# Stage 3 of a four-stage network: pairs finished one step on, merges two turns on, copies out of PSUM on ScalarE, the substitution of diagonal blocks on GpSimd

## The chip, the cores and the metric

The kernel runs on one core of a Trainium2 chip. The metric is the device time of one execution in microseconds (us), the median of several. A profile of one execution, taken by the hardware profiler, stands beside it. The engines are PE (TensorE matmuls; PEld are its weight loads), DVE (VectorE), ACT (ScalarE), POOL (GpSimd) and SP (SyncE, which here issues nearly all DMAs). Each engine works through its own queue in order.

## What is computed

The network has two layers of two blocks each, all in float32, on 2048 tokens of width 512 (4 sequences of 512): a state-space block, a mixture of experts, a gated delta rule ("stage 3", all that is changed here), and a sequence-routed mixture. Stage 3, cut to what matters:

```python
q = silu(conv(x @ Wq))            # causal depthwise conv of 4 taps
k = silu(conv(x @ Wk)) * D ** -0.5
v = silu(conv(x @ Wv))            # 16 heads of 128
alpha, beta = sigmoid(x @ Wa + ba), sigmoid(x @ Wb + bb)
def step(St, inp):                # one token; the state is 128x128 a head
    q_, k_, v_, a_, b_ = inp
    err = einsum('bhij,bhj->bhi', St, k_) - v_
    Sn = a_ * St - b_ * err * k_  # outer product of err and k_
    return Sn, einsum('bhij,bhj->bhi', Sn, q_)
o = layernorm(o) * ln_w + ln_b    # each head apart
o = o * sigmoid(x @ Wg)
y = o @ Wo
x = x + layernorm(y)
```

## The kernel before

The kernel computes the recurrence in chunks of 128 tokens. A **step** of stage 3 is one pair of heads of one sequence of 512 tokens (4 chunks): 8 pairs times 4 sequences are 32 steps, and the loop at the end of `delta_rule` runs once more to drain. Inside a chunk the recurrence is a triangular system; its 128x128 matrix is inverted by blocks of 32. The pieces, generators that give up control at each `yield`, are:

- `prepare(h, ...)`, once a head: the projections k, q and v (`project`, L151: each four products over the 512 inputs, which the trace shows as eight MATMULs of 512 columns), each followed by `conv_silu` (L156 to L163): ACT writes the last tap and the bias to `cv`, DVE adds three taps reading the projection `p` in PSUM (L158), ACT takes the sigmoid (L162), POOL multiplies (L163). Then come the masked products `lt` and `pt` (L672, L675), and the diagonal blocks of `lt` go to DRAM (L679); last `kq`, `gc` and `kt` (L685 to L694).
- `solve(blocks, yi)`: all 32 diagonal blocks of the pair (2 heads, 4 chunks, 4 blocks) come back from DRAM laid out over 128 partitions (`lb`, L710), are inverted by forward substitution, 31 rounds of a multiply (L720, into `term`) and an add (L727, into `xb`), and go by DRAM into `yi` (L732, L736).
- `merge(lts, yi)`: from the inverted diagonal blocks to the whole inverse. Three DVE transposes of `yi` (L752 to L754), then four rounds of small products on PE (L760, L772 and L780, L793, L801), each followed by copies.
- `recur(heads, yi, o)`: for each of the 4 chunks, products in PSUM tag `sq` (L817): `r` (copied out by ACT, L830), `u` (copied out by DVE, L840), the new state `S` (DVE, L847 and L850), the output `o` (ACT, L858).
- `finish(o, ...)`, not a generator: statistics of `o` (DVE L114 and L115, POOL L117 and L118), `normalise` (DVE, L122), then for each head the gate projection (L151, from `wg`), its sigmoid `gt` (L892), four PE transposes of `o` (L895), scaling into `oT` (L897) and the product with `gt` (POOL, L898), then 16 MATMULs with `wo` (L903) whose sums are added to `y` (L909).

Step n of the loop issues `prepare` of pair n (both heads) in turns with `merge` of pair n-1, then `solve` of pair n in turns with `recur` of pair n-1, and then `finish` of pair n-1 as a whole. After a sequence's last pair, `residual` (statistics, `normalise`, POOL addition, L147) follows.

The order on each engine's queue is not the program's. It is fixed when the program is built, by a planner that takes instructions as their inputs and buffers come free by its own estimates, and prefers the earlier in the program among those. A tile's buffers are shared by tag, `bufs` of them: PSUM has three for `mm` (projections, `lt`, `pt`, gates, `wo` sums), three for `tr` (transposes, merges) and two for `sq` (the recurrence). `cv` and `sg` have two buffers each, `o` and `gt` one. The two inverses `yi0` and `yi1` take turns, and `lt`, `pt`, `vT`, `kq`, `kt` and `gc` have four buffers, two pairs' worth.

Of the kernel before, what the change touches and what calls it, by code (L numbers as in the profile page):

```python
# [16 lines left out]
P = 128  # L17
# [59 lines left out]
def network(ctx: ExitStack, tc: tile.TileContext, a: dict, out: bass.AP):  # L77
# [75 lines left out]
    def conv_silu(pool, dst, p, w, bias):  # L153

        cv = pool.tile([P, S], F32, tag="cv", name="cv", bufs=2)
        nc.scalar.activation(cv, p, AF.Identity, bias=bias, scale=w[:, 3:4])  # L156
        for j in range(1, 4):
            nc.vector.scalar_tensor_tensor(  # L158
                cv[:, j:], p[:, : S - j], w[:, 3 - j : 4 - j], cv[:, j:], ALU.mult, ALU.add
            )  # L160
        sg = pool.tile([P, S], F32, tag="sg", name="sg", bufs=2)
        nc.scalar.activation(sg, cv, AF.Sigmoid)  # L162
        nc.gpsimd.tensor_tensor(dst, cv, sg, ALU.mult)  # L163
# [417 lines left out]
    def delta_rule():  # L581
        with (
# [22 lines left out]
            def decays(xT):  # L605

                zp = ps("sq")[:H2, :]
                project(zp, lambda k: wab[:, k, 0:H2], xT)
                al = bp.tile([H2, TPB, CP], F32, tag="al", name="al")
                nc.gpsimd.memset(al[:, :, 0:1], 0.0)  # L610
                nc.scalar.activation(al[:, :, 1:], chunk(zp), AF.Sigmoid, bias=ba)
                ga = bp.tile([H2, TPB * CP], F32, tag="ga", name="ga")
                flat = al.rearrange("h c t -> h (c t)")
                nc.vector.tensor_tensor_scan(ga, flat, c("pad1")[:H2], 0.0, ALU.mult, ALU.add)
                dd = dram.tile([2, H2, TPB * CP], F32, tag="dd", name="dd")
                nc.sync.dma_start(dd[0], flat)
                nc.sync.dma_start(dd[1], ga)
                bps = ps("sq")[:, : TPB * H2]
                for i in range(TPB):
                    dst = bps[:, i * H2 : (i + 1) * H2]  # L620
                    for k in range(KD):
                        nc.tensor.matmul(
                            dst,
                            lhsT=xT[:, k, i * P : (i + 1) * P],
                            rhs=wab[:, k, H2:],
                            start=k == 0,
                            stop=False,
                        )
# [5 lines left out]
                nc.vector.tensor_scalar(nb, nb, -1.0 / P, None, ALU.mult)  # L634
                return dd, nb

            def prepare(h, w, xT, dd, nb, blocks, out):
# [5 lines left out]
                for j, dst in ((1, qk[:, 0, :]), (0, qk[:, 1, :]), (2, vT)):  # L643
                    p = ps("mm")
                    project(p, lambda k: w[:, k, j, :], xT)
                    conv_silu(sp, dst, p, cw[:, j, h, :], cb[:, j, h : h + 1])
                    yield
# [56 lines left out]
            def solve(blocks, yi):  # L704
# [11 lines left out]
                for i in range(BK - 1):  # L716
# [3 lines left out]
                    nc.vector.tensor_tensor(  # L720
# [6 lines left out]
                    nc.vector.tensor_tensor(rest, rest, term, ALU.add)  # L727
# [10 lines left out]
            def merge(lts, yi):  # L738
# [10 lines left out]
                lo, hi = slice(0, 2 * BK), slice(2 * BK, P)  # L749
                xx = sp.tile([P, UNITS, 2 * BK], F32, tag="xx", name="xx", bufs=1)  # L750
# [56 lines left out]
            def recur(heads, yi, o):  # L807

                st = None
                for cc in range(TPB):  # L810
# [29 lines left out]
                    nc.vector.tensor_copy(  # L840
# [40 lines left out]
            def finish(o, ws, wos, pair, xT, y):  # L881
# [5 lines left out]
                gated = []  # L887
                for j in range(2):
                    p = ps("mm")
                    project(p, lambda k: ws[j][:, k, :], xT)  # L890
                    gt = sp.tile([P, S], F32, tag="gt", name="gt", bufs=1)
                    nc.scalar.activation(gt, p, AF.Sigmoid)  # L892
                    p = ps("tr")
# [4 lines left out]
                    nc.gpsimd.tensor_tensor(oT, oT, gt, ALU.mult)  # L898
                    gated.append(oT)
                for i in range(TPB):  # L900
# [7 lines left out]
                    else:  # L908
                        nc.vector.tensor_tensor(y[i], y[i], p, ALU.add)  # L909

# [14 lines left out]
            before = None  # L925
            for n in range(B * NPAIR + 1):
                b, pair = divmod(n, NPAIR)
                now, parts, heads = None, [], []
                if n < B * NPAIR:
                    if pair == 0:  # L930
# [3 lines left out]
                        y = [  # L934
                            bp.tile([P, D], F32, tag=f"y3{i}", name=f"y3{i}") for i in range(TPB)
                        ]
# [9 lines left out]
                    now = (heads, inverses[n % 2], b, pair, xT, y)  # L946
# [246 lines left out]
```

## Time and profile before

| quantity | value |
|---|---|
| time, median of 3 runs | 3653.46 us (3652.5 to 3656.45) |
| the profiled execution | 3652.81 us, of which span 3651.0 us |
| busy in the span | PE 3179.4, PEld 1752.8, DVE 2064.8, ACT 799.0, POOL 953.5 us |
| one regular step of stage 3 (1987.2 to 2052.2) | 65.0 us: PE 59.27, DVE 44.88, ACT 15.86, POOL 19.74 busy |
| the next step (2052.2 to 2117.1) | 64.9 us: PE 59.18, DVE 44.82, ACT 15.87, POOL 19.73 busy |
| three steps round a change of sequence (1639 to 1857) | 147.0 and 71.0 us |
| mean granted clock of TensorE | 0.907 |

The span runs from the first to the last instruction. Stage 3 begins before 1200 us (the first MATMUL with `wh` is at 1190.2) and its last output `o` is written at 3366. A busy time is a sum of instruction durations; a PE that waits with an instruction started still counts as busy. The granted clock is the share of full clock that the chip gave TensorE in a stretch.

### The profile page before, as it was taken

The numbers are of one execution on the slowest core, as the hardware profiler recorded it, in microseconds if no ns is written. First come the engines' busy times: TensorE is split into PE (matmuls) and PEld (weight loads), VectorE is DVE, ScalarE is ACT, GpSimd is POOL, SyncE is SP. The second block draws the span as 40 slices with busy tenths as digits, with TensorE's granted clock in tenths as the row PEclk, the third lists the DMA queues.
The fourth block names the chain that finished last, engine by engine and source line by source line (L and its number), as shares of the span: only waits on it lengthen the run. The fifth ranks groups of instructions, "written<-read, shape, count | busy, mean of one in ns | idle before, by whom it ended". The sixth has DMA issues, their size and how long they took to land.

```text
span 3651.0 us, 39495 instructions
## 1 busy us (share of the span) xinstructions
PE 3179.4 (87%) x13779; PEld 1752.8 (48%) x13779; DVE 2064.8 (57%) x5189; ACT 799.0 (22%) x1399; POOL 953.5 (26%) x1018
## 2 busy tenths in 40 slices
PE   7889989899995889989989989889899989897268
PEld 3333344455552455555555645555555545555123
DVE  4556441311125667676766666766676767664852
ACT  2223211111110222222222222222222222221111
POOL 1322120300016323322423222323223323221112
PEclk9889989999997889989989989989999989998679
DMA  6000010389973322322322322323322323220300
GB/s 239 0 1 0 0 50 0 137 285 319 319 262 93 81 63 60 90 60 54 82 63 64 89 59 53 83 60 80 73 60 64 78 60 77 69 60 22 107 12 35
DMA packets 281240, 316.23 MB, mean 87 GB/s; under 512 B 119073, under 2 KB 184993, under 8 KB 281042
## 3 DMA queue, kind: packets, MB, share of 16 engines
q1 hardware_dynamic: 266496, 277.62, 26.7%
q10 hardware_dynamic: 9426, 19.31, 1.4%
q0 software_dynamic: 5120, 16.78, 1.4%
q8 instruction: 110, 1.80, 0.2%
q14 instruction: 88, 0.72, 0.1%
HBM read 271.95 MB, written 41.68 MB: 86 GB/s over the span
## 4 chain that ended last, share of the span: by engine, by line
PE 75%; DVE 12%; POOL 6%; issue 3%; ACT 3%; DMA 2%; SPq 0%; POOLq 0%; ACTq 0%; DVEq 0%
PE mm L151 32%; PE sq L817 7%; PE mm L903 7%; PE mm L512 5%; PE mm L672 3%; PE sq L534 3%; PE sq L276 2%; POOL rs L118 2%; PE tr L358 2%; PE sq L1086 2%; DVE o L122 2%; DVE prod L997 2%; DVE term L720 1%; DVE st L114 1%; DVE xb L727 1%
## 5 line engine op out<-in xcount | busy, mean ns | idle before, releaser
L151 PE MATMUL mm<-xT,wh 128*128 128x512 f32 x1536 | 691.2, 607 | 2.2 <-DVE cv L158 2.0
L158 DVE SCALAR_TENSOR_TENSOR cv<-mm,prm,cv 128x511 f32<-128x511 f32 (+2 forms) x672 | 499.3, 744 | 289.2 <-ACT cv L156 275.1
L151 PEld LDWEIGHTS mm<-xT,wh 128*128 128x128 f32 x1536 | 294.4, 194 | 364.8 <-issue 357.6
L903 PE MATMUL mm<-wo,oT 128*128 128x512 f32 x512 | 293.9, 738 | 60.0 <-POOL oT L898 60.0
L156 ACT ACTIVATE cv<-mm,prm 128x512 f32<-128x512 f32 x224 | 172.6, 771 | 524.1 <-PE mm L151 516.7
L720 DVE TENSOR_TENSOR term<-lb,xb 128x60 f32<-128x60 f32 (+24 forms) x992 | 257.7, 260 | 20.5
L151 PE MATMUL mm<-xT,wg 128*128 128x512 f32 x512 | 262.2, 600 | 0.7 <-ACT gt L892 0.7
L727 DVE TENSOR_TENSOR xb<-xb,term 128x60 f32<-128x60 f32 (+24 forms) x992 | 223.7, 226 | 24.7
L903 PEld LDWEIGHTS mm<-wo,oT 128*128 128x128 f32 x512 | 120.0, 242 | 216.8 <-issue 139.2
L163 POOL TENSOR_TENSOR qk<-cv,sg 128x512 f32<-128x512 f32 x128 | 162.5, 1269 | 201.5 <-ACT sg L162 201.4
L895 PE MATMUL tr<-const,o 128*128 128x128 f32 x256 | 101.8, 467 | 111.9 <-DVE o L122 111.1
L162 ACT ACTIVATE sg<-cv 128x512 f32<-128x512 f32 x224 | 140.4, 627 | 256.6 <-DVE cv L158 255.6
L512 PE MATMUL mm<-gu,rT 128*128 128x352 f32 x624 | 190.9, 459 | 0.2 <-ACT rT L508 0.2
L151 PE MATMUL mm<-xT,gu 128*128 128x512 f32 (+1 forms) x384 | 176.2, 618 | 12.6 <-DVE act L353 12.6
L512 PEld LDWEIGHTS mm<-gu,rT 128*128 128x128 f32 x624 | 118.2, 190 | 76.5 <-issue 17.8
L817 PE MATMUL sq<-S,kq 128*128 128x128 f32 x768 | 154.5, 283 | 0.0
L117 POOL TENSOR_SCALAR rs<-mv 128x1 f32<-128x1 f32 (+2 forms) x112 | 30.9, 276 | 449.1 <-DVE mv L115 448.9
L672 PE MATMUL mm<-qk 128*128 128x128 f32 x1024 | 137.8, 283 | 6.3 <-POOL vT L163 2.9
L276 PE MATMUL sq<-w_out,G 128*128 128x512 f32 x256 | 128.0, 651 | 13.4 <-POOL G L272 11.7
L546 POOL DMA_INDIRECT got<-yg,index x32 | 38.1, 1189 | 362.5 <-DMA yg<-yo 345.4
L163 POOL TENSOR_TENSOR vT<-cv,sg 128x512 f32<-128x512 f32 x64 | 100.2, 1565 | 115.3 <-ACT sg L162 115.3
L672 PEld LDWEIGHTS mm<-qk 128*128 128x128 f32 x1024 | 123.9, 194 | 11.0 <-POOL vT L163 3.1
(231 smaller groups left out, 4891.2 us busy)
## 6 DMA issues: line engine op xcount, KB each, us to landing
gu<-in_gu SPq DMA_DIRECT2D x86, 704.0 KB
wh<-in_wh SPq DMA_DIRECT2D x64, 768.0 KB
ag<-dd SPq DMA_DIRECT2D x64, 516.0 KB
dn<-in_dn SPq DMA_DIRECT2D x43, 512.0 KB
wg<-in_wg SPq DMA_DIRECT2D x64, 256.0 KB
wo<-in_wo SPq DMA_DIRECT2D x64, 256.0 KB
lb<-blocks SPq DMA_DIRECT2D x128, 128.0 KB
xg<-zero SPq DMA_DIRECT2D x3, 3328.0 KB
```

What stands on the lines that cost most here:

```text
L151: nc.tensor.matmul(dst, lhsT=w(k), rhs=xT[:, k, :], start=k == 0, stop=k == n - 1)
L156: nc.scalar.activation(cv, p, AF.Identity, bias=bias, scale=w[:, 3:4])
L158: nc.vector.scalar_tensor_tensor(cv[:, j:], p[:, : S - j], w[:, 3 - j : 4 - j], cv[:, j:], ALU.mult, ALU.add)
L162: nc.scalar.activation(sg, cv, AF.Sigmoid)
L163: nc.gpsimd.tensor_tensor(dst, cv, sg, ALU.mult)
L276: nc.tensor.matmul(po, lhsT=G[ct][:, i * P : (i + 1) * P], rhs=w_out[:, ct, :], start=ct == 0, stop=ct == NCT - 1,)
L512: nc.tensor.matmul(dst, lhsT=rT[:, k, :], rhs=gu[:, k, lo : lo + F], start=k == 0, stop=k == KD - 1)
L672: nc.tensor.matmul(one(p, cc), lhsT=one(kT, cc), rhs=one(rhs, cc), start=True, stop=True)
L720: nc.vector.tensor_tensor(term, lb[:, i : i + 1, i + 1 :].to_broadcast([P, n, left]), xb[:, :n, i : i + 1].to_broadcast([P, n, left]), ALU ...
L727: nc.vector.tensor_tensor(rest, rest, term, ALU.add)
L817: nc.tensor.matmul(p[:, j, :], lhsT=lhsT, rhs=rhs, start=n == 0, stop=n == len(terms) - 1,)
L903: nc.tensor.matmul(p, lhsT=one(gated[j], i), rhs=wos[j], start=j == 0, stop=j == 1)
```

## The change

It does six things to stage 3 and nothing to the others:

1. `finish` becomes a generator that starts a step later. In step n it takes part, first in each turn, in the phase of `prepare` of pair n and `merge` of pair n-1, for pair n-2: a turn for each gate projection, one for the transposes and products, two for the `wo` sums, with the `residual` of a sequence's last pair inside them. The statistics and the normalisation of `o` (`centred`) stay at the end of the step. The loop runs once more, `o` and `gt` get two buffers, and the loads of `wg` and `wo` are issued after those of `wh`.
2. `merge` gives up its first two turns.
3. `conv_silu` in stage 3 (`apart=True`) first copies the projection out of PSUM by ACT into the `sg` buffer; the three DVE taps read that copy, and the sigmoid overwrites it afterwards.
4. The copy of `u` goes from DVE to ACT.
5. The 31 multiplies and 31 adds of the substitution go from DVE to POOL.
6. For room, `al` and `ga` of `decays` share the two `xn` buffers, and the four `y` tiles are taken when a sequence's first pair is finished.

```diff
-    def conv_silu(pool, dst, p, w, bias):
+    def conv_silu(pool, dst, p, w, bias, apart=False):
         cv = pool.tile([P, S], F32, tag="cv", name="cv", bufs=2)
+        sg = pool.tile([P, S], F32, tag="sg", name="sg", bufs=2)
+        if apart:
+            nc.scalar.copy(sg, p)
+            p = sg
         nc.scalar.activation(cv, p, AF.Identity, bias=bias, scale=w[:, 3:4])
...
-        sg = pool.tile([P, S], F32, tag="sg", name="sg", bufs=2)
         nc.scalar.activation(sg, cv, AF.Sigmoid)
...
-                al = bp.tile([H2, TPB, CP], F32, tag="al", name="al")
+                al = bp.tile([H2, TPB, CP], F32, tag="xn", name="al", bufs=2)
...
-                ga = bp.tile([H2, TPB * CP], F32, tag="ga", name="ga")
+                ga = bp.tile([H2, TPB * CP], F32, tag="xn", name="ga", bufs=2)
...
-                    nc.vector.tensor_tensor(
+                    nc.gpsimd.tensor_tensor(
                         term,
...
-                    nc.vector.tensor_tensor(rest, rest, term, ALU.add)
+                    nc.gpsimd.tensor_tensor(rest, rest, term, ALU.add)
...
                 lo, hi = slice(0, 2 * BK), slice(2 * BK, P)
+                for _ in range(2):
+                    yield
                 xx = sp.tile([P, UNITS, 2 * BK], F32, tag="xx", name="xx", bufs=1)
...
-                    nc.vector.tensor_copy(
+                    nc.scalar.copy(
                         u, pair(lambda j, vT, pt, kq, gc, kt: [(yi[:, j * TPB + cc, :], r[:, j, :])])
...
-            def finish(o, ws, wos, pair, xT, y):
+            def centred(o):
                 rows = [(cc, j) for cc in range(TPB) for j in range(2)]
                 mv, rs = stats([o[:, cc, j, :] for cc, j in rows], EPS / P, "o")
                 for n, (cc, j) in enumerate(rows):
                     normalise(o[:, cc, j, :], o[:, cc, j, :], mv, rs, n)
-                gated = []
+
+            def finish(o, ws, wos, b, pair, xT, y):
+                gates = []
                 for j in range(2):
                     p = ps("mm")
                     project(p, lambda k: ws[j][:, k, :], xT)
-                    gt = sp.tile([P, S], F32, tag="gt", name="gt", bufs=1)
+                    gt = sp.tile([P, S], F32, tag="gt", name="gt", bufs=2)
                     nc.scalar.activation(gt, p, AF.Sigmoid)
+                    gates.append(gt)
+                    yield
+                gated = []
+                for j in range(2):
                     p = ps("tr")
...
-                    nc.gpsimd.tensor_tensor(oT, oT, gt, ALU.mult)
+                    nc.gpsimd.tensor_tensor(oT, oT, gates[j], ALU.mult)
                     gated.append(oT)
+                yield
                 for i in range(TPB):
...
+                    if pair == NPAIR - 1:
+                        residual(bp, b * TPB + i, y[i])
+                    if i % 2:
+                        yield
...
-            before = None
-            for n in range(B * NPAIR + 1):
+            before = last = None
+            for n in range(B * NPAIR + 2):
...
                 if before:
-                    gates = gate_weights(before[3])
                     parts.append(merge([head[0] for head in before[0]], before[1]))
+                if last:
+                    if last[2] == 0:
+                        y = [
+                            bp.tile([P, D], F32, tag=f"y3{i}", name=f"y3{i}") for i in range(TPB)
+                        ]
+                    o, at, of, x_of = last
+                    parts.insert(0, finish(o, *gate_weights(of), at, of, x_of, y))
                 in_turns(*parts)
-                parts = []
+                parts, last = [], None
...
-                    o = sp.tile([P, TPB, 2, P], F32, tag="o", name="o", bufs=1)
+                    o = sp.tile([P, TPB, 2, P], F32, tag="o", name="o")
                     parts.append(recur([head[1] for head in before[0]], before[1], o))
                 in_turns(*parts)
                 if before:
-                    finish(o, *gates, *before[3:])
-                    if before[3] == NPAIR - 1:
-                        for i in range(TPB):
-                            residual(bp, before[2] * TPB + i, before[5][i])
+                    centred(o)
+                    last = (o, *before[2:])
                 before = now
```

More of the change, by code (lines that the diff above doesn't have):

```diff
@@ L645, in prepare @@
                     project(p, lambda k: w[:, k, j, :], xT)
-                    conv_silu(sp, dst, p, cw[:, j, h, :], cb[:, j, h : h + 1])
+                    conv_silu(sp, dst, p, cw[:, j, h, :], cb[:, j, h : h + 1], apart=True)
                     yield
@@ L933, in delta_rule @@
                         dd, nb = decays(xT)
-                        y = [
-                            bp.tile([P, D], F32, tag=f"y3{i}", name=f"y3{i}") for i in range(TPB)
-                        ]
                     blocks = dram.tile([2, TPB, NB, BK, BK], F32, tag="blocks", name="blocks")
@@ L945, in delta_rule @@
                         parts.append(prepare(h, w, xT, dd, nb, blocks[j], heads))
-                    now = (heads, inverses[n % 2], b, pair, xT, y)
+                    now = (heads, inverses[n % 2], b, pair, xT)
                 if before:
-                    gates = gate_weights(before[3])
                     parts.append(merge([head[0] for head in before[0]], before[1]))
+                if last:
[5 more added lines that the diff above has]
+                    parts.insert(0, finish(o, *gate_weights(of), at, of, x_of, y))
                 in_turns(*parts)
-                parts = []
+                parts, last = [], None
                 if now:
```

## The prediction

> **What bounds the kernel now.** I read the page's busy line first, then the busy times of stretches of one regular step of stage 3, then the timeline where PE goes idle, then the groups by shape.
>
> ```profile
> PE 3179.4 (87%) x13779; PEld 1752.8 (48%) x13779; DVE 2064.8 (57%) x5189; ACT 799.0 (22%) x1399; POOL 953.5 (26%) x1018
> core 0: us, PE busy (x) PEld busy (x) DVE busy (x) ACT busy (x) POOL busy (x), PEclk, DMA share, GB/s
> 1987.20:2034.40 47.20, 46.79 (x299) 29.93 (x297) 30.68 (x76) 13.31 (x25) 15.26 (x16) 1.00 0.41 98
> 2034.40:2038.00 3.60, 0.18 (x3) 0.02 (x1) 1.79 (x12) 0.50 (x2) 1.90 (x2) 0.88 0.02 6
> 2038.00:2043.10 5.10, 3.21 (x9) 1.45 (x9) 4.93 (x20) 1.47 (x3) 1.26 (x1) 0.50 0.01 3
> 2043.10:2047.40 4.30, 4.30 (x5) 1.84 (x6) 3.69 (x13) 0.57 (x1) 1.31 (x1) 0.50 0.00 0
> 2047.40:2052.20 4.80, 4.80 (x13) 2.11 (x12) 3.79 (x14) 0.00 (x0) 0.00 (x0) 1.00 0.00 0
> ```
>
> Columns: stretch, length, then busy us of PE, PEld, DVE, ACT, POOL, the granted clock, the DMA share. The reader is to see that PE is the limit for 47.2 us of the 65.0 (46.79 busy, full clock), and that the other 17.8 us are `finish`: 3.6 us idle, then 9.4 us at half clock, then the rest. The timeline (start, length, what; in brackets the idle time before and what ended it) names the waits:
>
> ```profile
> 2035.88 1.67 POOL L118 TENSOR_TENSOR rs<-rs,mhalf 128x8 f32<-128x8 f32 x1
> 2037.99 3.24 PE L895 MATMUL tr<-const,o 128*128 128x128 f32 x8 [3.42 <-DVE o L122]
> 2043.09 1.22 PE L903 MATMUL mm<-wo,oT 128*128 128x512 f32 x1 [1.87 <-POOL oT L898]
> 2041.78 1.26 POOL L898 TENSOR_TENSOR oT<-oT,gt 128x512 f32<-128x512 f32 x1 [4.23 <-ACT oT L897]
> 2041.91 1.22 DVE L720 TENSOR_TENSOR term<-lb,xb 128x75 f32<-128x75 f32 x1
> ```
>
> PE waits for statistics and normalisation (3.42), paces its transposes by DVE (3.24), waits for the product with the gate (1.87). The last two lines are another fact: a DVE multiply of two SBUF inputs, 0.21 us alone, takes 1.22 when a POOL product has just begun, and ends with it.
>
> ```profile
> L118 POOL TENSOR_TENSOR rs<-rs,mhalf 128x8 f32<-128x8 f32 x32 | 53.3, 1666 | 2.7
> L651 POOL TENSOR_TENSOR d<-const,nb 128x516 f32<-128x516 f32 x64 | 67.1, 1049 | 130.2 <-DVE nb L634 70.2 <-DVE m L658 60.1
> L689 POOL COPY gc<-ag 128x4 f32<-128x4 f32 x64 | 12.0, 188 | 249.7 <-DVE S L850 233.0 <-DMA ag<-dd 15.0 <-DVE term L720 0.2
> L117 POOL TENSOR_SCALAR rs<-mv 128x8 f32<-128x8 f32 x32 | 7.7, 240 | 255.5 <-DVE mv L115 255.5
> L131 ACT COPY xT<-tr 128x512 f32<-128x512 f32 x48 | 27.1, 587 | 226.0 <-PE tr L130 225.7
> ```
>
> These rows (total busy, mean ns, idle before) are my prices for operations that move.
>
> [...] 0.50 follows the idle 3.42 us in every step I looked at. [...] L651 gives 1049/516 = 2.0, and I use that.
>
> **The change, part by part, for a regular step of 65.0 us.**
>
> *Finish a step later, with two `gt`.* The work stays the same: 8 transposes and 16 `wo` MATMULs. In the full-clock stretch 128-column MATMULs start 0.11 us apart and 512-column ones 0.43, so they need 8 x 0.11 + 16 x 0.43 = 7.8 us against 17.8 now: a **gain of 10.0**, leaving PE 47.2 + 7.8 = **55.0 us**. The gate projections already lie inside `recur` in this trace and only change place; under `recur` the next step's first projections can lie, since `mm` has three buffers. The normalisation, 8 x 0.34 us of DVE and 1.9 of POOL, is no longer waited for by PE but still blocks DVE's queue (taps, `lt` behind it) if POOL answers late. The loads of `wg` and `wo`, 4 of 256 KB, pass behind `wh` on SP; they were waiting for their buffers anyway, and about 40 us of cover remain: 0, and if it went, at most some us.
>
> *Copies on ACT.* Six copies of 587 ns (L131) and four of 372 instead of DVE's 422: ACT goes from 15.9 to 15.9 + 3.5 + 1.5 = 20.9 us: hidden, far under 55. PSUM is free earlier, but the copy now waits for one of two `sg` buffers, which POOL's product frees. `u` on ACT can queue behind a 0.77 us activation; four times, up to 3 us on `recur`'s chain, hidden while PE has projections to do, 0 to 3 if not. DVE loses 1.7.
>
> *The taps* now have two SBUF inputs: 18 a step at 0.747 = 13.4 us[...].
>
> *Substitution on POOL.* It leaves DVE: (257.7 + 223.7)/32 = 15.0 us a step; DVE falls to 44.9 - 15.0 - 1.7 = 28.2. On POOL it is 62 dependent instructions. The elements are the sum of (i//4+1)(31-i) over 31 rounds = 1560, so 50 an instruction. None this small with two inputs is in the trace. Low: 0.188 of the 4-element copy and nothing for elements but 0.05: 0.24. High: L118, whose 1, 4 and 8 elements take 571, 1040 and 1666, has 0.41 fixed, plus 50 x 2.0 ns: 0.51. I take 0.20, between L689 and L117, plus 0.10 = **0.30**: 18.6 us a step.
>
> [...] POOL's other work is 18.8 us a step (medians: four products of 1.26 for `qk`, two for `vT`, two for `oT`, 4 x 0.90, 2 x 1.05, 1.9, and 1.1 of small ones). DVE's holders are 13.4 of taps, two scans of 1.22 and 8 normalisations of 0.34 = 18.6. Sum 18.8 + 18.6 + 18.6 = **56.0**; before it was 18.8 + 5.2 + 12.8 = 36.8. With 3 us for hand-overs and queues standing at a wait (POOL's for `sg`, for `lb` to land), **59.0 us**. That is above PE's 55.0[...].
>
> *Merges two turns on.* Nothing is added; the inverse gets about two projections' turns more to arrive. Today the chain is: blocks leave at 2017.6, the substitution starts at 2029.95 and ends at 2054.1, `xx` is transposed at 2061.8, so 12.3 + 24.1 + 7.7 us. On POOL the middle becomes 62 x 0.38 (0.08 between two dependent POOL instructions, L117 to L118) = 24 alone, 35 to 45 with other POOL work[...]. Behind a late `xx` stand the taps on DVE and everything on PE. With two buffers of `yi` there is room for it: 0.
>
> *`al`, `ga` in `xn`, `y` late, residual inside `finish`.* Four times in all; the 147 + 71 us round a change of sequence are 23 above three regular steps. The residual's waits get cover: 0 to 8 us gained each of three times, a small loss possible if `al` waits for `xn`; I take 10 in all.
>
> **Sum.** The last pair's finish stays bare, so 31 x (65.0 - 59.0) = 186, plus 10: 196. From the profiled 3652.8 (span 3651.0 and 1.8 around it; the median of runs is 0.7 higher): 3652.8 - 196 + 0.7 = about **3458 us**.
>
> **The rivals.**
>
> *A, PE stays the bound* (0.22). If a small POOL instruction costs 0.24, [...] PE's 55.0 rules: 31 x 10.0 + 10 gives 3333. [...] Against it: 55.0 leaves no slack for any wait.
>
> *B, POOL's substitution delays the inverse: slower* (0.24). Place: between `lb` and L752. If the planner queues `merge` before the next pair's `lt`, a period is 12.3 + substitution + 7.7 + some 8 for the merge; it passes 65 once the substitution spans over 37 us. The same comes[...] once an instruction costs over (65.0 - 3 - 37.4)/62 = 0.40. At a span of 39, 67 us a step: + 62, so 3715[...]. For it: in-order queues, 62 dependent instructions on an engine that also serves every projection. Against: the two turns' delay and two buffers.
>
> *C, the gain is eaten up* (0.09): the finish's stall goes, and DVE's stand behind POOL's statistics returns about as much; within 3600 to 3660, centred on 3640. It includes that the planner, which sets the order, does not in effect move the work: PE would keep an idle over 3 us and half-clock stretches at every step.
>
> **How the numbers follow.** My forecast has 0.45 and holds 57 to 63 us a step: 31 x 8 or 31 x 2 us less and 10 for the changes of sequence, about 3395 to 3580. With A's 3333 below and B's milder form above, the range is 3335 to 3715; only B's extreme and a step under 55 are left out. This kernel can tell some 0.2% from no change. Faster: 0.45 + 0.22 + 0.03 of C = 0.70; same 0.04 (C); slower 0.02 + 0.24 = 0.26.
>
> **What would show it.** In a regular step of the new profile: no idle of PE before L895 by DVE, L903's mean down from 738 to about 600 ns, clock 1.00 through the step (first part right); POOL busy near 45 us a step and DVE's term and xb rows gone (substitution right); L158's mean above 747 and POOL rows above their medians[...]. If PE is busy over 95% with a step near 55, A holds; if PE or DVE idles for L752 or for `lt`, and a POOL instruction of L727 takes over 0.40, B. A step over 65 or under 57 makes the forecast wrong.

## The result, and the profile after

The change makes the kernel **slower: 3810.39 us** (median of 4 runs, 3808.59 to 3821.31) against 3652.98 for the kernel before beside it, a ratio of 1.0435 (95% interval 1.0414 to 1.0456). The forecast was 3458, with a range that ended at 3715. The execution profiled took 3821.31 us (the longest of the four) with a span of 3819.5, 168.5 us more than the span before; from the second `lt` of the first step to that of the last are 163.2 us more, so nearly all of it lies in the 31 intervals between. A regular step takes 68 to 75 us (70.6 on average, from one second `lt` to the next) where it took 65.0.

The page's busy line, and the busy times of one regular step (columns as before: stretch, length, then PE, PEld, DVE, ACT, POOL, the granted clock, DMA share):

```profile
PE 3190.7 (84%) x13779; PEld 1784.3 (47%) x13779; DVE 1737.0 (45%) x3077; ACT 957.1 (25%) x1719; POOL 1583.1 (41%) x3002
core 0: us, PE busy (x) PEld busy (x) DVE busy (x) ACT busy (x) POOL busy (x), PEclk, DMA share, GB/s
1488.10:1556.90 68.80, 58.65 (x323) 35.22 (x322) 34.86 (x66) 20.85 (x39) 39.29 (x82) 0.93 0.28 68
```

The work moved where it was to go: DVE from 44.9 to 34.9 us a step (28.2 were forecast), POOL from 19.7 to 39.3, ACT to 20.9. No engine is full, and yet the step is longer. The timeline of that step, where PE is idle before its transposes of `o` (start, length, what; idle time before and what ended it):

```profile
1525.77 0.24 POOL L117 TENSOR_SCALAR rs<-mv 128x8 f32<-128x8 f32 x1
1526.10 1.67 POOL L118 TENSOR_TENSOR rs<-rs,mhalf 128x8 f32<-128x8 f32 x1
1527.73 1.26 POOL L167 TENSOR_TENSOR qk<-cv,sg 128x512 f32<-128x512 f32 x1
...
1527.80 3.88 DVE L122 TENSOR_SCALAR o<-o,mv,rs 128x128 f32<-128x128 f32 x8 [12.29 <-POOL rs L118]
...
1529.13 0.47 PE L908 MATMUL tr<-const,o 128*128 128x128 f32 x1 [6.87 <-DVE o L122]
```

It is the same wait as in the kernel before (PE for the normalised `o`), and longer: 6.87 us, not 3.42. DVE itself stands 12.29 us for the statistics on POOL, with the next projections' taps behind it in its queue. And POOL is not late with the 1.9 us of statistics: their input `mv` is written at 1514.82, and it starts them at 1525.77, in the moment when the last round of the substitution ends (1499.6 to 1525.8). They stand behind the rounds in POOL's queue, and the product of the next pair's `qk` stands behind them.

The groups (total busy, mean ns, idle before): first the taps and the substitution with all their shapes together, then the normalisation, the transposes that wait for it, and rows that were the prediction's prices:

```profile
L163 DVE SCALAR_TENSOR_TENSOR cv<-sg,prm,cv 128x511 f32<-128x511 f32 (+2 forms) x576 | 553.0, 964 | 266.3 <-ACT cv L161 242.7 <-POOL term L724 9.1 <-POOL qk L167 6.4
L731 POOL TENSOR_TENSOR xb<-xb,term 128x60 f32<-128x60 f32 (+24 forms) x992 | 316.2, 319 | 74.7
L724 POOL TENSOR_TENSOR term<-lb,xb 128x60 f32<-128x60 f32 (+24 forms) x992 | 302.8, 305 | 232.1 <-DMA lb<-blocks 163.5
```

```profile
L122 DVE TENSOR_SCALAR o<-o,mv,rs 128x128 f32<-128x128 f32 x256 | 110.6, 502 | 357.0 <-POOL rs L118 357.0
...
L908 PE MATMUL tr<-const,o 128*128 128x128 f32 x256 | 82.5, 435 | 225.9 <-DVE o L122 221.5
...
L655 POOL TENSOR_TENSOR d<-const,nb 128x516 f32<-128x516 f32 x64 | 68.1, 1064 | 313.1 <-DVE m L662 272.1 <-DVE nb L638 41.0
...
L118 POOL TENSOR_TENSOR rs<-rs,mhalf 128x8 f32<-128x8 f32 x32 | 53.4, 1670 | 2.3
...
L131 ACT COPY xT<-tr 128x512 f32<-128x512 f32 x48 | 27.4, 586 | 241.2 <-PE tr L130 241.2
...
L693 POOL COPY gc<-ag 128x4 f32<-128x4 f32 x64 | 14.7, 230 | 12.2 <-DMA ag<-dd 10.5 <-DVE S L856 1.7
```

In the kernel before, the taps, the normalisation and the transposes were:

```profile
L158 DVE SCALAR_TENSOR_TENSOR cv<-mm,prm,cv 128x511 f32<-128x511 f32 (+2 forms) x672 | 499.3, 744 | 289.2 <-ACT cv L156 275.1
...
L122 DVE TENSOR_SCALAR o<-o,mv,rs 128x128 f32<-128x128 f32 x256 | 86.3, 339 | 53.6 <-POOL rs L118 53.6
...
L895 PE MATMUL tr<-const,o 128*128 128x128 f32 x256 | 101.8, 467 | 111.9 <-DVE o L122 111.1
```

The substitution's instructions take 0.305 and 0.319 us, as priced. The taps, with two inputs in SBUF, went from 0.744 to 0.964 us. The operations used as prices take about what they took, but for the copy of four elements (188 to 230 ns). But DVE now waits 357.0 us for the statistics in all, where it waited 53.6.

What closes the step is in the chain of waits, which follows each instruction back to what released it. One turn of it, from the statistics of one step to the substitution of the next (start, length, what; the main links):

```profile
3147.66 1.69 POOL rs L118
3149.37 3.89 DVE o L122 x8
3153.26 0.66 DVE cv L163
...
3158.10 1.10 DVE cv L163
3159.22 1.33 DVE cv L163
3160.58 1.65 DVE cv L163
...
3170.97 3.28 PE mm L676 x16
...
3179.99 0.70 DVE lt L679
...
3182.01 4.77 DMA blocks<-lt
...
3188.41 2.92 DMA lb<-blocks
```

Then come the rounds, 3191.5 to 3217.7, and behind them in POOL's queue the next statistics. The circle adds up to the step: 1.7 + 3.9 us of statistics and normalisation, 17.7 of taps and the ACT instructions between them (3153.3 to 3171.0), 9.0 to the start of the second `lt`, 11.5 until the blocks are back, 26.2 of rounds: 70.0. TensorE is in it with some 6.5 us. The two numbers to remember are those 17.7 and 26.2; the experiments tell what lengthens them.

### The profile page after: what moved, and what is told of

It reads as the page before. It is cut to its first block, busy times and chain, and to the rows that moved or that the text cites. A ratio compares the mean times of both kernels' runs of the same rounds, so it can differ in the third digit from the quotient of the medians.

```text
span 3819.5 us, 39622 instructions
## 1 busy us (share of the span) xinstructions
PE 3190.7 (84%) x13779; PEld 1784.3 (47%) x13779; DVE 1737.0 (45%) x3077; ACT 957.1 (25%) x1719; POOL 1583.1 (41%) x3002
## 5 line engine op out<-in xcount | busy, mean ns | idle before, releaser
L151 PE MATMUL mm<-xT,wh 128*128 128x512 f32 x1536 | 756.6, 628 | 1.4 <-ACT sg L159 0.7
L163 DVE SCALAR_TENSOR_TENSOR cv<-sg,prm,cv 128x511 f32<-128x511 f32 (+2 forms) x576 | 553.0, 964 | 266.3 <-ACT cv L161 242.7
L724 POOL TENSOR_TENSOR term<-lb,xb 128x60 f32<-128x60 f32 (+24 forms) x992 | 302.8, 305 | 232.1 <-DMA lb<-blocks 163.5
L731 POOL TENSOR_TENSOR xb<-xb,term 128x60 f32<-128x60 f32 (+24 forms) x992 | 316.2, 319 | 74.7
L122 DVE TENSOR_SCALAR o<-o,mv,rs 128x128 f32<-128x128 f32 x256 | 110.6, 502 | 357.0 <-POOL rs L118 357.0
L908 PE MATMUL tr<-const,o 128*128 128x128 f32 x256 | 82.5, 435 | 225.9 <-DVE o L122 221.5
L917 PE MATMUL mm<-wo,oT 128*128 128x512 f32 x512 | 261.2, 646 | 5.2 <-POOL oT L911 4.2
L159 ACT COPY sg<-mm 128x512 f32<-128x512 f32 x192 | 112.3, 585 | 413.2 <-POOL qk L167 256.4
L167 POOL TENSOR_TENSOR qk<-cv,sg 128x512 f32<-128x512 f32 x128 | 164.9, 1289 | 122.0 <-ACT sg L166 122.0
L655 POOL TENSOR_TENSOR d<-const,nb 128x516 f32<-128x516 f32 x64 | 68.1, 1064 | 313.1 <-DVE m L662 272.1
L908 PEld LDWEIGHTS tr<-const,o 128*128 128x128 f32 x256 | 47.3, 203 | 274.5 <-DVE o L122 261.7
L161 ACT ACTIVATE cv<-sg,prm 128x512 f32<-128x512 f32 x192 | 155.2, 809 | 3.9
```

Of the source, the lines that this page charges most:

```text
L122: nc.vector.tensor_scalar(dst, src, mv[:, j, 0:1], rs[:, j : j + 1], ALU.subtract, ALU.mult)
L151: nc.tensor.matmul(dst, lhsT=w(k), rhs=xT[:, k, :], start=k == 0, stop=k == n - 1)
L163: nc.vector.scalar_tensor_tensor(cv[:, j:], p[:, : S - j], w[:, 3 - j : 4 - j], cv[:, j:], ALU.mult, ALU.add)
L724: nc.gpsimd.tensor_tensor(term, lb[:, i : i + 1, i + 1 :].to_broadcast([P, n, left]), xb[:, :n, i : i + 1].to_broadcast([P, n, left]), ALU ...
L731: nc.gpsimd.tensor_tensor(rest, rest, term, ALU.add)
L917: nc.tensor.matmul(p, lhsT=one(gated[j], i), rhs=wos[j], start=j == 0, stop=j == 1)
```

## The experiments

Ratios are to the kernel before, run beside each, with 95% intervals. Unless said, the edit is to the changed kernel. The kernel before took 3652.5 to 3660.1 us in the different sets, so differences under some 8 us across sets say nothing.

**Which of the parts: substitution and copies, taken back singly and together.**

```diff
 e1: substitution on VectorE again
-                    nc.gpsimd.tensor_tensor(term, ...); nc.gpsimd.tensor_tensor(rest, rest, term, ALU.add)
+                    nc.vector.tensor_tensor(term, ...); nc.vector.tensor_tensor(rest, rest, term, ALU.add)
 e3: no copy of the projections, taps read PSUM again
-                    conv_silu(sp, dst, p, cw[:, j, h, :], cb[:, j, h : h + 1], apart=True)
+                    conv_silu(sp, dst, p, cw[:, j, h, :], cb[:, j, h : h + 1])
 e5: both.   e4: no substitution.   e13: no substitution and no copies
-                for i in range(BK - 1):
+                for i in range(0):
```

> The changed kernel with the substitution's 62 instructions back on DVE, everything else of the change kept. Theory Q (POOL's queue: the statistics of o and the products of the next pair's projections stand behind the substitution): the loss goes as a whole, no wait of DVE for L118 over 3 us, a step of 55 to 60 us, 3390 to 3520 us in all. Theory P[...]: the taps still read two SBUF inputs but against 18.8 us of POOL work a step instead of 38[...], so also under 60 us a step; this run does not tell Q from P, it tells whether the substitution's place is the whole loss. Theory L (the inverse itself arrives late and holds up what stands behind the transposes of merge): the chain is 2 us shorter than on POOL, so a step of 66 to 69, 3700 to 3780.

> The changed kernel with the taps of conv_silu reading PSUM as before (no copy on ACT); the substitution stays on POOL. Theory Q: the statistics and products still stand behind the substitution; 3770 to 3850. Theory P: [...] the step falls to 57 to 61 us: 3450 to 3540. Theory L: the substitution alone is some 2 us shorter, 3730 to 3800.

> The changed kernel with both moves between engines undone: the substitution on DVE and the taps reading PSUM without a copy; the later finish, the later merges and u on ACT stay. If the two moves are the whole loss, the finish's gain shows: a step of 56 to 60 us, 3380 to 3520. If the later finish gives nothing by itself: 3600 to 3660.

> The changed kernel with the 31 rounds of the substitution left out (the diagonal blocks' inverses stay unit matrices; all DMAs, merges and the recurrence remain). It gives the floor without that work. All theories: PE sets the step at 55 to 57 us, 3330 to 3400; Theory P adds that the taps stay over 0.80 us in the mean, because POOL's products still contend with them.

> Leaves out all 31 rounds of the substitution (its result is not computed), and the taps read PSUM again. What is left is the later finish[...]. T1, the later finish does take 10 us of a step's 65 from TensorE once nothing holds GpSimd: a step of 55 to 57 us, 3380 to 3440 us. T2, TensorE keeps most of its 10 us of stalls at the new place of the finish even so (its own turns and halved clock): a step of 59 to 61 us, 3470 to 3540 us.

Measured, medians in us with the ratio's interval (e4 and e13 do not compute the inverse):

| taps read | no substitution | substitution on VectorE | substitution on GpSimd |
|---|---|---|---|
| PSUM | e13: 3329.34 [0.9088, 0.9118] | e5: 3604.73 [0.9846, 0.9879] | e3: 3600.72 [0.9826, 0.9873] |
| SBUF copies | e4: 3473.91 [0.9473, 0.9534] | e1: 3703.69 [1.0104, 1.0138] | the change: 3810.39 [1.0414, 1.0456] |

Read by rows and columns: the copies cost 145 us without a substitution, 99 with it on VectorE, 210 with it on GpSimd. Moving the substitution costs 107 us with the copies and nothing (3601 against 3605) without. **Without the copies the change is 1.5% faster than the kernel before.** With neither, in e13, a regular step is 54.4 us: the 55.0 of TensorE that the prediction worked out.

Few of these times lie where they were expected. e1 falls into the range of a late inverse (Theory L), but not for that reason: PE waits 27 us in all for `xx` there. e5 falls where a later finish that gives nothing was put, which e13 refutes. e3 fits none of its three theories: the copies were worth more than POOL's queue alone allowed, and less than Theory P had it (3450 to 3540). e4 lies above its range, by what the copies cost it, and e13 somewhat below. A step of e3 is 63 us. Here are one of them, with no engine full (columns as before), and two long waits (engine, line, waited for: us in total, times, longest):

```profile
1467.00:1529.80 62.80, 57.43 (x323) 34.65 (x322) 31.20 (x64) 17.03 (x33) 35.55 (x82) 0.95 0.30 74
```

```profile
DVE o L122 <- POOL rs L118: 295.2, 32, 13.0
...
PE tr L908 <- DVE o L122: 150.6, 61, 10.3
```

The groups of e13 that answer to the finish:

```profile
L917 PE MATMUL mm<-wo,oT 128*128 128x512 f32 x512 | 245.5, 614 | 5.8 <-DVE lt L679 3.3 <-POOL oT L911 2.4
L908 PE MATMUL tr<-const,o 128*128 128x128 f32 x256 | 38.1, 292 | 6.9 <-DVE o L122 6.9
```

The idle time before the transposes of `o` is 6.9 us in all, against 225.9 in the changed kernel. With the merges two turns on, the later finish does what it was to do, if nothing holds the statistics.

**The taps' second input, or the copy itself?** e11 makes the copy and lets ACT's bias step read it, but the taps read PSUM; e10 gives `sg` a third buffer.

```diff
 e11
         if apart:
             nc.scalar.copy(sg, p)
-            p = sg
-        nc.scalar.activation(cv, p, AF.Identity, bias=bias, scale=w[:, 3:4])
+        nc.scalar.activation(cv, sg if apart else p, AF.Identity, bias=bias, scale=w[:, 3:4])
 e10
-        sg = pool.tile([P, S], F32, tag="sg", name="sg", bufs=2)
+        sg = pool.tile([P, S], F32, tag="sg", name="sg", bufs=3 if apart else 2)
```

> The changed kernel where the copy of the projection into the sg buffer is made and read by ACT's bias step as now, but the three taps on DVE read the projection in PSUM. ACT's work and the time for which sg is held stay, PSUM is held longer[...]. The copies cost about 210 us (the changed kernel at 3810 against 3601 with the taps reading PSUM and no copy). Theory P[...]: near the kernel without copies, 3600 to 3660. Theory B (sg, two buffers, is held from the copy to POOL's product, and the copies lengthen the chain of a projection): 3730 to 3810.

> The changed kernel with three sg buffers in stage 3 instead of two, all else the same: taps still read the copy in SBUF. Theory B: the copy no longer waits for a product two projections back, and most of the 210 us come back, 3620 to 3700. Theory P: the taps stay as slow as in the changed kernel (L163 mean 0.95 to 1.0 us), 3780 to 3815.

e11: 3614.23 us (0.9877 to 0.991), so the copy itself costs some 14 us, and the taps' reading of SBUF the other 196. e10: 3821.2 us (1.0443 to 1.0477), no gain, though ACT's wait for the `sg` buffer (256.4 us in the changed kernel) is gone from its waits: taking that wait away gained nothing. The taps' rows of e4 (no substitution) and e3 (no copies), with e3's rounds, show the lengthening by itself:

```profile
L163 DVE SCALAR_TENSOR_TENSOR cv<-sg,prm,cv 128x511 f32<-128x511 f32 (+2 forms) x576 | 533.7, 927 | 307.5 <-ACT cv L161 292.4 <-POOL qk L167 6.4
```

```profile
L163 DVE SCALAR_TENSOR_TENSOR cv<-mm,prm,cv 128x511 f32<-128x511 f32 (+2 forms) x672 | 498.8, 743 | 304.1 <-ACT cv L161 293.0
...
L731 POOL TENSOR_TENSOR xb<-xb,term 128x60 f32<-128x60 f32 (+24 forms) x992 | 280.9, 283 | 72.2
L724 POOL TENSOR_TENSOR term<-lb,xb 128x60 f32<-128x60 f32 (+24 forms) x992 | 272.7, 275 | 220.0 <-DMA lb<-blocks 148.9
```

The taps take 927 ns beside POOL's other work alone, 964 with the rounds too, and 743 from PSUM. The source alone does not do it: in the changed kernel's trace the 153 of its 576 SBUF taps that overlap no POOL instruction take 747 ns on average, and the 423 that overlap one take 1043. Nor does the overlap alone: in the kernel before, the 441 of the 672 taps from PSUM that overlap a POOL instruction take 747 as well. The rounds pay too, 0.305 and 0.319 us against 0.275 and 0.283 in e3: 171 of their 1984 instructions last over 0.5 us, each of them beside a tap from SBUF; in the rounds of e3's chain (3007.6 to 3031.5 and 3079.5 to 3094.2) none lasts over 0.34. How the two engines hold each other up, the traces do not show. In the chain both stretches lie on the circle: the taps' part is 17.7 us where e3's chain has 13.8 (3037.39 to 3051.19), the rounds' part 26.2 where it is 24.0. Together these are 6.1 of the 6.8 us a step that lie between the two kernels (210.5 us over the 31 intervals from one second `lt` to the next).

**The substitution alone, in the kernel before.** e2 moves it to POOL and changes nothing else; e15 leaves it out.

> The kernel before with the substitution alone moved to POOL. Theory Q (POOL's queue): the statistics of o stand behind the substitution in the middle of the finish that PE waits for, so 5 to 15 us more a step: 3800 to 4150. If only the taps' reading of SBUF makes the move to POOL expensive (Theory P): within 40 us of before, 3620 to 3700.

> The kernel before with all 31 rounds of the substitution left out (its result is not computed). The prediction took the finish on TensorE as what bounds a step of the kernel before. T1, that holds, 47.2 + 17.8 us of TensorE are there without a substitution as well: 3630 to 3660 us. T2, the circle of waits with the substitution in it sets the 65.0 us, and the stall of the finish lies beside it: 3350 to 3560 us.

e2: 3888.15 us (1.0625 to 1.066), as the theory of POOL's queue had it. With the finish at its old place the rounds stand ahead of the statistics that PE waits for. From its waits:

```profile
PE tr L895 <- DVE o L122: 271.5, 32, 9.8
...
DVE o L122 <- POOL rs L118: 231.2, 32, 8.7
```

Before, these are 111.1 and 53.6. e15: 3576.11 us (0.9776 to 0.9809), between the ranges of the two theories; a regular step is 63.0 to 64.8 us where it was 65.0. PE's wait for the normalised `o` is still there:

```profile
PE tr L895 <- DVE o L122: 106.2, 32, 4.2
```

So in the kernel before, leaving out the whole substitution is worth 77 us, a third of it in the first step (29.1 us in place of 55.6), and the regular step stays nearly as long: its bound was the finish, as the prediction had it. With the finish out of the way the same substitution is worth 271 (e13 to e3).

**The merges two turns on.** e14 is the kernel before with the later finish alone: e5 without the two turns and with the copy of `u` on DVE.

```diff
 e14, against e5
-                for _ in range(2):
-                    yield
-                    nc.scalar.copy(
+                    nc.vector.tensor_copy(
                         u, pair(...)
```

> The kernel before with the later finish alone: substitution and the copy of u on VectorE, taps on PSUM, merges not held back by two turns. T1, the held-back merges and the copy of u are worth nothing, as the prediction had it: 3590 to 3620 us, as with them (3605). T2, the two turns are what the later finish needs, since the solved blocks now come later: 3640 to 3720 us. T3, they cost, because the merge then lands where projections have run out: 3500 to 3580 us.

3947.08 us (1.0776 to 1.0812), 342 more than e5 and above all three ranges. In its waits:

```profile
PE tr L764 <- DVE xx L756: 375.3, 29, 21.6
```

With the finish moved, PE runs into the merge before the inverse has come and stands up to 21.6 us. In e5 these waits are 7 us in all. So the two turns make the later finish usable. (The copy of `u` changed with them; it was not tried alone.) Four turns add nothing:

> Taps on PSUM, substitution on GpSimd (3601 us so far), and the merge held back four turns in place of two. In TensorE's queue the first merge products then stand behind the second lt of the next pair and not before it. Theory T1, the step is a closed circle of waits (lt to the blocks, substitution, transposes into xx, merge, next lt: 10.7 + 24.0 + 6.5 + 21.6 = 62.8 us), so that taking lt out from behind the merge opens it: the step falls to 55 to 58 us, near the 54.4 of the kernel without a substitution, and the time to 3360 to 3450 us. Rival T2, the loads on GpSimd and VectorE hold the step and not their order: 3580 to 3620 us. Rival T3, the merge then stands bare in front of the recurrence: 3650 to 3800 us.

> The same with the substitution on VectorE (3605 us so far with two turns, 3947 with none). T1, the circle of waits: 3360 to 3460 us, about the same as with the substitution on GpSimd. T2, the loads: 3590 to 3620 us. T3, the bare merge: 3650 to 3800 us.

> The change as it is (copies, substitution on GpSimd, 3810 us), with four turns in place of two. T1, the copies cost their 210 us by stretching the same circle (taps and queues at GpSimd ahead of lt): opening it gives most of that back, 3400 to 3560 us. T2, the copies cost[...], whatever the order: 3560 to 3640 us, the gain of the other kernel (e16) less their 6.7 us a step. T3, nothing is gained: 3790 to 3850 us.

e16, on e3: 3606.73 (0.9854 to 0.9887). e17, on e5: 3609.47 (0.9872 to 0.9905). e18, on the change: 3835.93 (1.0488 to 1.0523), 26 us worse. In e3 the merge's first products stand in PE's queue before `wo` sums whose addition to `y` comes ahead of the second `lt` on DVE; in e16 they stand behind these sums, and the step is still 62.5 us. So the circle through `xx` and the merge to the next `lt` is not what holds the step. PE's whole wait for `xx` in e3 is 8 us. The first two results lie where the rival put them that no order changes anything; it is taken up again below.

**POOL's queue.** e6 ties rounds 16 to 30 behind the statistics of `o` in POOL's queue (which are now called as the last turns of `recur`); e12 does so with the taps on PSUM.

```diff
 e6, e12
-        nc.gpsimd.tensor_tensor(rs, rs, mhalf.to_broadcast([P, n]), ALU.pow)
+        ins = nc.gpsimd.tensor_tensor(rs, rs, mhalf.to_broadcast([P, n]), ALU.pow)
+        if tag == "o":
+            ahead.append(ins.ins)
...
+                    with tc.issue_after(ahead[-1]) if ahead else nullcontext():
                         (the two instructions of a round)
```

> The changed kernel with one difference in POOL's queue: rounds 16 to 30 of the substitution are queued behind the statistics of o (L117, L118 of the changed kernel), which so come about halfway through it instead of at its end; no work is added or removed. Theory Q: DVE's wait for the statistics (357 us in all in the changed kernel, 11 a step) falls under 2 us a step and PE's wait for the normalisation with it, the wait of ACT's copy for the product on POOL stays; the step falls from 69 to 71 us to 63 to 67, 3620 to 3740 in all. Theory P: [...] within 20 us of 3810. Theory L: the inverse arrives 2 us later, 3810 to 3870.

> The change with both reliefs at once: the taps read PSUM again (no copy), and rounds 16 to 30 of the substitution stand behind the statistics of o in GpSimd's queue. Theory T1, what is left of TensorE's stall is its wait for the normalised o, held by those statistics: the 6.7 us a step before and within the transposes of o go, a step falls from 62.8 to some 56 to 58 us, and the time from 3601 to 3400 to 3470 us. Rival T2, GpSimd's queue only makes something else late, the product with the gate or the solved blocks, as it did with the copies in place (36 us gained of the same 200): 3550 to 3600 us.

e6: 3774.25 us (1.0301 to 1.0343), 36 better than the change and outside its three ranges. e12: 3655.3 us (0.9988 to 1.0005), 55 worse than e3 and outside both ranges. DVE's long wait for `rs` is gone from e6, and others came (in e6 L171 is the product that is L167 elsewhere, L918 is L911, L924 is L917, L763 is L758):

```profile
ACT sg L163 <- POOL qk L171: 303.4, 65, 9.9
PEld mm L924 <- POOL oT L918: 270.9, 58, 9.9
...
DVE xx L763 <- DMA yi<-solved: 191.1, 32, 17.8
```

The product with the gate now stands behind the second half of the rounds, and the inverse is late: in the change DVE's wait for `yi` was 21 us in all. e19 goes further: with taps on PSUM and four turns, rounds 20 to 30 stand behind the next pair's last `q` product, and the transposes into `xx` behind its second `pt`. e20 adds the copies.

```diff
 e19, e20
+        ahead[:] = [nc.gpsimd.tensor_tensor(dst, cv, sg, ALU.mult).ins]     # conv_silu
...
+            def solve_rest(lb, xb, yi, wait):       # in the next step's first turns
+                for i in range(EARLY, BK - 1):      # EARLY = 20
+                    with tc.issue_after(ahead[-1]) if wait else nullcontext():
+                        rounds(lb, xb, i)
```

> Taps on PSUM, substitution on GpSimd, merges four turns on (3607 us before this), and now rounds 20 to 30 of the substitution stand in GpSimd's queue behind the next pair's two k and two q products, and the transposes into xx on VectorE behind its second lt and pt. Theory T1, the step is a circle of waits through GpSimd's queue: lt to lb 11 us, the substitution 24, and from its end 27.6 to the next second lt, because the statistics of o and the products that lead to that lt stand behind it; with 20 rounds in the circle it is 11 + 20 x 0.77 + 27.6 = 54 us, the merge comes some 5 us late: a step of 56 to 60 us, 3390 to 3530 us. Rival T2, it is the load of GpSimd[...], which no order changes: 3580 to 3640 us. Rival T3, the late merge takes everything back: 3540 to 3620 us with TensorE idle ahead of the merge's first products and no longer ahead of the transposes of o.

> The same with the copies of the projections (taps on SBUF), as in the change: 3836 us with four turns alone. T1, most of the copies' cost was the substitution's circle stretched by longer taps: with it opened they cost what they cost without any substitution, 3474 less 3329 = 145 us: 3540 to 3680 us. T2, [...] whatever the order: over 200 us above the kernel without copies, 3700 to 3840 us.

e20: 3744.87 us (1.021 to 1.0273), 91 better than the same with the rounds in one piece (e18, 3835.93), most of its regular steps 65 to 66 us in place of 71. The moved rounds are some 10 us long. So with the copies the place of the rounds in the queue does count, by about half of their length; the time is still in the range of T2 and not of T1. e19: 3646.41 us (0.9962 to 0.9988), 40 worse than e16 and outside its three ranges, with steps from 58 to 74 us. Its chain shows the next circle: last round, `solved` and `yi` through DRAM, `xx`, merge, the recurrence, the product behind which the rounds wait, the first rounds, the statistics and the next taps, the rest of the rounds. It takes 61.6 us (from one transpose into `xx` at 3101.40 to the next at 3163.00).

e3 has two such circles. Its chain goes once through `lt` as in the changed kernel, 53 us of it (2998.58 to 3051.19), and in the next step through PE:

```profile
3077.51 0.64 ACT sg L166
...
3078.22 1.27 POOL qk L167
...
3094.53 1.68 POOL rs L118
...
3096.24 2.61 DVE o L122 x3
...
3101.31 8.52 PE mm L151 x16
3109.82 3.43 PE mm L917 x8
3113.26 3.63 PE mm L676 x32
```

From 3079.5 to 3094.2 the chain is rounds that stand behind that `qk` product in POOL's queue, and the statistics stand behind the rounds; then come the normalised `o`, PE's work in order with merge and recurrence (to 3140.3), and the next such product at 3141.00: 62.8 us.

**Load without the chain.** e21 executes the rounds on a tile of zeros, with nothing that waits for them (the blocks are not loaded; the merge gets unit blocks).

> Taps on PSUM, substitution on GpSimd, merges two turns on (3601 us), but the 31 rounds no longer belong to the chain: they work on a tile of zeros instead of the loaded blocks, the load of the blocks is left out, and the merge gets unit blocks in place of their result. So the inverse is not computed; GpSimd executes the same 62 instructions a step, which wait for nothing and which nothing waits for. Without the rounds it is 3329 us. Theory T1, the 272 us are dependences (the wait for the blocks and the work queued behind the rounds): 3329 to 3430 us. Theory T2, they are the load on GpSimd[...]: 3560 to 3620 us. In between, the share of each is read off.

3806.94 us (1.0402 to 1.0437), and no answer to the question: as the rounds need not wait for anything, the planner put those of all 32 steps into the first seven. Five of these take 117 to 137 us each, with POOL 112.9 of 136 us busy. One of the five, and one of the later steps:

```profile
core 0: us, PE busy (x) PEld busy (x) DVE busy (x) ACT busy (x) POOL busy (x), PEclk, DMA share, GB/s
1500.00:1636.00 136.00, 66.94 (x327) 39.30 (x326) 31.60 (x65) 17.84 (x35) 112.90 (x357) 0.71 0.12 30
2300.00:2354.40 54.40, 54.40 (x323) 33.72 (x322) 31.36 (x65) 16.96 (x33) 18.28 (x20) 1.00 0.30 73
```

It shows once more that a step without rounds is 54.4 us of PE at full clock; what the rounds cost as load alone, spread evenly, stays open. Against load alone speaks only that the same work in another order moves the time (e20 to e18 by 91 us, e12 to e3 by 55).

## Why the prediction was wrong, step by step

- **"PE ... 55.0"** for the later finish: right as a floor. e13 and the late steps of e21 measure 54.4, and L917 falls to 614 ns ("to about 600"). In the changed kernel it is not reached; the "idle of PE before L895 by DVE" that was to go is still there, 225.9 us in all, twice what it was.
- **"0.30 us" for an instruction of the substitution:** right, 0.305 and 0.319 in the change, 0.275 and 0.283 in e3. "62 x 0.38 = 24 alone" meets e3's 24.0 by luck: one starts 0.36 us after another there, so 22 alone, and other POOL work is 2.5 of the 24.0. "35 to 45 with other POOL work" was too much (26.2), and so was "POOL busy near 45" (39.3).
- **The failed step is the sum of 56.0 and "3 us for hand-overs and queues standing at a wait".** It adds POOL's time to that of DVE's "holders" (taps, scans, normalisations), as if no two of these ever ran together, and takes the total for the length of the step. That they take turns was the author's estimate, and the traces do not show it; they show the longer taps and rounds above. Without the taps its own sum is 56.0 - 13.4 = 42.6, so that PE's 55.0 would set the step; yet e3's is 63, with POOL busy for 35.6 us of it and PE for 57.4. By the chain, what sets it is a circle through queues worked in order. The wait was named ("if POOL answers late", behind it "taps, `lt`") and given no cost; it is 12.29 us of DVE in the step above. The 3 us of waiting stand for what was 70.0 - 56.0 = 14.0.
- **"Copies on ACT ... hidden" and "The taps ... 13.4":** mis-sized. ACT had the room (e11: 14 us), but 13.4 was the taps' length undisturbed, counted once as load. The taps lengthen to 0.964 us and the rounds with them (0.305 and 0.319), and in the chain both lie on the circle: 210 us in all, some 7 a step. This alone turns a gain of 1.5% into a loss of 4.3%, and it is 210 of the 352 us by which the forecast missed.
- **"Merges two turns on ... 0":** right as a cost of the change, which has the turns; wrong as a picture of it, since once the finish is later, the two turns and the copy of `u` together are worth 342 us (e14).
- **Changes of sequence, "10 in all":** no gain. The two intervals round one are 165 us, 23 over two regular ones, where they were 152 and 22 over.
- **Rival B** had the sign and the amount (3715 and more) and the wrong place, so that its amount is luck. It put the loss in a late inverse, decided by "a span of over 37 us": the span is 26.2, and moving the merge (e16 to e18) gains nothing. Its other form needed over 0.40 us for an instruction; they took 0.305 and 0.319. What waits in the trace is what stands behind the rounds in POOL's queue: statistics and products, not `xx`. Its sum of 12.3 + span + 7.7 + 8 would have given 54 us here. **Rival A's** bound is real and was not reached; **C** named the right wait (DVE's stand behind POOL's statistics), but let it only cancel the gain (3640).

Shown by runs: the cost of the taps' input, the finish's floor, what the substitution costs once the finish is later (271 us), the worth of the turns with the copy of `u`, and that the rounds' place in the queue counts where the copies are. Read from the chain and not separately proved: that the circles named hold the change at 70 us and e3 at 63. The rival, that the rounds cost by load and not by order, was put to the test in e21 and not decided. No order tried here opened all the circles at once; e5, with the substitution spread through DVE's queue, ends at the same 62.5, and why so near is open.

The best version measured that computes the result is e3, the change without the copies: 3600.72 us, 1.5% below the kernel before and 5.5% below the change.

## What to carry to other kernels

When a chain of small dependent instructions moves to another engine, list what stands behind it in that engine's queue and follow each of those to the chain's own next start: if the path closes, the step cannot be shorter than it, however idle the engines are (here 70.0 us, with PE busy for 58.65 of a step's 68.80 and POOL for 39.29). Adding up busy times gives a floor only. Before an input is copied from PSUM to SBUF to free a buffer, ask whether its reader then has two SBUF inputs beside a busy GpSimd: here such a tap took 1043 ns beside a POOL instruction and 747 without one.

## What the hardware showed that was not expected

- A two-input GpSimd instruction of about 50 elements takes 0.28 us, and one that depends on it starts 0.36 us after it (e3).
- A quarter more for the taps from SBUF (743 to 927 ns) came beside POOL's ordinary products already, before any of the substitution was on POOL (e4).
- The normalisation of `o` takes 339 ns a tile before, where no POOL instruction overlaps it, and 502 in the change. In the change it begins within 0.1 us of a POOL product in 23 of 32 steps, and its first two instructions then take 1.28 and 1.06 us (3.88 us for eight in the timeline above); those that no POOL instruction overlaps take 337 ns.
